# The first loads of a two-layer MoE and LoRA kernel: one queue in place of two, and 32 constant products ahead of the first real one in place of 27

## The chip, the cores and the metric

One core of one Trainium2 chip runs the kernel. The metric is the device time in microseconds (us); lower is better. Where several runs are given, the middle one counts.

## What is computed

`x` has 2 samples of 1024 tokens and 256 channels, in float32. Two layers are added to it one after the other. The first is a mixture of experts: per sample the router takes the 2 best of 8 experts, each an MLP with gelu and a hidden size of 1024, and a shared MLP is added. The second is a linear layer with a low-rank part, mixed from 8 pairs of matrices.

```python
def mlp(x, g, u, d):
    return (gelu(x @ g) * (x @ u)) @ d          # 256 -> 1024 -> 256, tanh gelu

w, sel = top_k(softmax(cond_8), 2)              # one row per sample
w = w / w.sum(-1)
x = x + sum(w[e] * mlp(x, skill_gate[e], skill_up[e], skill_down[e]) for e in sel) \
      + mlp(x, shared_gate, shared_up, shared_down)
x = x + x @ W_base.T + b_base + 2.0 * sum(cond_8[e] * (x @ As[e].T) @ Bs[e].T for e in range(8))
```

## The kernel before

The work on TensorE is done in float32 split into two parts: a high part rounded to the matmul's type (`hi_of`, L177) and the rest (`lo_of`, L180). Each product of two float32 matrices is then three matmuls, high by high, low by high and high by low, summed in PSUM. The first layer is cut into groups: for each of the 2 samples and each of its 3 MLPs (shared, first expert, second expert) there are 4 pieces of 256 hidden units, 24 groups in all. In a group the gate and the up matrix are each a matrix of 2 by 2 blocks (A11, A12, A21, A22), and so is the sample's x (B11, B12, B21, B22; the second index is the half of the tokens). Groups 1 to 23 use a scheme with seven block products in place of eight (`block_product`, L288). Group 0 uses the plain eight (`plain_product`, L299), because they need no sums of blocks before TensorE can begin: first A11 with B11 into the banks ps_ag and ps_au (six matmuls of 128x512, gate and up in turn), then A21 with B11 into ps_dg and ps_du (six), then A12 and A22 with the second block of x, which is named P2, and so on with B12 and P3. After gelu and the product with the up half, `down` (L346) multiplies by the down weights and sums into four banks `y`.

The order of all work is written by hand. `at` (L105) puts a step with a time into a list, `MOVED` shifts single steps by their place in the list, and L621 sorts by time and place and issues them. Each engine then runs its steps in exactly that order. So the time of a step is only its place in the queues of the engines it uses: a load's place is that on SP's or ACT's queue of DMA issues, which are also in the order of the engine's other work.

The steps at about -30 are the beginning. `warm_up` (L430) issues `WARM` matmuls of 128x128 on a constant tile of ones, into a bank of `y` that is not in use yet. `gelu_table` (L172) runs one small activation on ACT so that its table of functions is loaded. `load_first` (L205) loads a piece of group 0's weights from a packed copy: block A11 (columns 0 to `G2`, 128 KB), then A21 (`3 * G2`), A12, A22, and at last the down weights (256 KB). `load_x` (L249) loads one block of x (256 KB): (0, 0) is B11, (1, 0) the one named P2, (0, 1) is B12 and (1, 1) is P3. In the kernel before, B11 is issued by ACT, ahead of the table load, and all others by SP. `load_w` (L193) loads group 1's weights (768 KB). At -1.0 and after it come the splits that the first products need: A11's high part on ACT (L178), its low part on DVE (L181), then B11's high and low part on DVE, then A21's and A12's in the same manner, then P2's.

Of the kernel before, what the change touches and what calls it, by code (L numbers as in the profile page):

```python
# [67 lines left out]
MOVED = {  # L68
    33: -9.6, 40: 1.5, 81: -2.9, 87: -31.6, 100: 6.0, 101: 5.6, 102: 1.2, 1584: 7.5, 1599: 3.6, 1605: 8.7,
}  # L70
WARM = 27
LEN = 22


# [13 lines left out]
def moe_then_lora(ctx: ExitStack, tc: tile.TileContext, x, cond, skill, shared, piece0, second, outT):  # L88

    nc = tc.nc  # L90
# [14 lines left out]
    def at(t, f, *args):  # L105
        plan.append((round(t + MOVED.get(len(plan), 0), 1), len(plan), f, args))
# [139 lines left out]

    xraw, xs = {}, {}

    def load_x(b, k, j, eng=nc.sync):  # L249
        xraw[b, k, j] = xr_ring.next()  # L250
        eng.dma_start(out=xraw[b, k, j], in_=x[b, j, k])

    def x_sum(b, i, eng):

# [174 lines left out]
    def warm_up():  # L429
        ones = nc.const_aps.tensor(1.0, [P, P], BF16)  # L430
        for _ in range(WARM):
            nc.tensor.matmul(y[0][0][:, 0:P], lhsT=ones, rhs=ones, start=True, stop=True)

    V, A, G = nc.vector, nc.scalar, nc.gpsimd
    at(-30, warm_up)
    at(-29.9, gelu_table)
    at(-30, load_first, 0, G2)
    at(-30, load_x, 0, 0, 0, A)
    at(-29.8, load_first, 3 * G2, 4 * G2)
    at(-29.7, load_first, G2, 2 * G2)  # L440
    at(-29.6, load_x, 0, 1, 0)
    at(-29.5, load_first, 2 * G2, 3 * G2)
    at(-29.4, load_x, 0, 0, 1)
    at(-29.3, load_x, 0, 1, 1)
    at(-29.25, load_first, 4 * G2, PW)
# [153 lines left out]
    b = B - 1  # L599
# [90 lines left out]
```

## Time and profile before

| what | value |
|---|---|
| median of 3 runs | 383.97 us (383.63, 383.97, 385.43) |
| the profiled execution's own time | 385.71 us |
| its span, from the first to the last instruction | 383.9 us |
| TensorE busy (PE) | 378.6 us, 99% of the span |
| VectorE busy (DVE) | 296.2 us, 77% |
| ScalarE busy (ACT) | 255.7 us, 67% |
| GpSimd busy (POOL) | 199.5 us, 52% |
| constant products (L432) | 27, from 0.76 us on |
| first real product (L307) | at 4.99 us |
| B11's load: issue on ACT's queue | 0.72 us, 0.40 long |
| A11's load: issue on SP's queue | 0.72 us; landed 2.90 later |

The profiled execution is one run, looked at closely by the hardware profiler; its times are in us from its first instruction. A line of the timeline has the start, the length, the engine, the line of the kernel, the operation, the tiles (what is written, then what is read), their size and the count; in brackets is how long the engine stood idle before it, and what ended that. PEld is TensorE's loading of the stationary operand, SPq and ACTq are the issues of DMAs on SP's and ACT's queue. A line "A <- B" among the waits says that A stood idle until B was done.

### The profile page before, as it was taken

To read this page: it belongs to the slowest core of one execution; us is meant where nothing else is said; L and a number is where in the kernel's file an instruction comes from. 1 tells how busy PE (TensorE), PEld (TensorE's weight loads), DVE (VectorE), ACT (ScalarE), POOL (GpSimd) and SP (SyncE) were. 2 spreads that over 40 slices of the span, in tenths; PEclk is the share of its full clock that TensorE was granted. 3 is DMA by queue.
4 is the path that set the end of the run, shared out by engine and by line. 5 is a ranking of instruction groups with operands and counts; after the bars stand their busy time and mean duration, and the time that the engine had idled before them with its cause. 6 is when DMAs were issued, how large, how long until landed. Compare 5 with 4: busy or idle time off the path is not lost.

```text
span 383.9 us, 4871 instructions
## 1 busy us (share of the span) xinstructions
PE 378.6 (99%) x1689; PEld 313.9 (82%) x1689; DVE 296.2 (77%) x421; ACT 255.7 (67%) x439; POOL 199.5 (52%) x215
## 2 busy tenths in 40 slices
PE   7999999999999999999999999999999999999996
PEld 6888888888888888888888888888888888888885
DVE  4998897687876899877798887668668668677586
ACT  3678886767766767857858767667668567576520
POOL 0566788777465474555545664654655555340100
PEclk9999999999999999999999999999999999999999
DMA  7621221120220222031241202202202202000014
GB/s 248 247 55 56 82 84 14 68 84 0 84 82 1 85 82 82 2 137 29 109 164 28 85 0 82 82 2 82 82 2 83 82 2 83 0 2 0 0 56 164
DMA packets 8087, 26.00 MB, mean 68 GB/s; under 512 B 1024, under 2 KB 2048, under 8 KB 8064
## 3 DMA queue, kind: packets, MB, share of 16 engines
q0 software_dynamic: 2304, 12.58, 10.2%
q1 hardware_dynamic: 5616, 12.86, 9.7%
q8 instruction: 13, 0.21, 0.2%
q10 hardware_dynamic: 144, 0.26, 0.2%
q14 instruction: 10, 0.08, 0.1%
HBM read 23.60 MB, written 2.10 MB: 67 GB/s over the span
## 4 chain that ended last, share of the span: by engine, by line
PE 98%; DMA 1%; DVE 0%; ACT 0%; issue 0%
PE y L356 34%; PE ps_au L285 17%; PE ps_ag L285 17%; PE ps_dg L285 13%; PE ps_du L285 13%; PE ps_dg L307 1%; PE ps_du L307 1%; DMA w_raw<-in_piece 1%; PE y L307 1%; PE ps_ag L307 1%; PE ps_au L307 1%; PE ps_dg L379 0%; DVE ge L424 0%; DVE wa L181 0%; ACT wa L178 0%; DVE x L178 0%
## 5 line engine op out<-in xcount | busy, mean ns | idle before, releaser
L356 PE MATMUL y<-acts,wd 128*128 128x512 f32 x576 | 146.3, 389 | 0.0
L356 PEld LDWEIGHTS y<-acts,wd 128*128 128x128 f32 x576 | 108.0, 188 | 22.4
L181 DVE TENSOR_TENSOR acts<-act,acts 128x512 fp32r<-128x512 f32 x96 | 66.2, 722 | 12.2 <-ACT acts L178 12.2
L181 POOL TENSOR_TENSOR wa<-w_raw,wa 128x512 fp32r<-128x512 f32 (+1 forms) x46 | 53.7, 1182 | 36.3 <-PE ps_dg L285 32.3
L220 POOL TENSOR_TENSOR sf<-w_raw 128x256 f32<-128x256 f32 x46 | 39.3, 855 | 52.5 <-ACT u_u L311 26.6
L178 ACT CAST acts<-act 128x512 fp32r<-128x512 f32 x96 | 57.6, 620 | 13.0 <-DVE act L334 8.2
L181 POOL TENSOR_TENSOR wd<-w_raw,wd 128x256 fp32r<-128x256 f32 x44 | 32.2, 752 | 52.7 <-ACT wd L178 52.5
L317 DVE TENSOR_TENSOR c_u<-ps_du,u_u 128x512 f32<-128x512 f32 x46 | 31.6, 686 | 32.3 <-PE ps_du L285 31.0
L334 DVE SCALAR_TENSOR_TENSOR act<-ge,gate_w,c_u 128x512 f32<-128x512 f32 x48 | 45.3, 943 | 3.4 <-ACT ge L326 1.4
L326 ACT ACTIVATE ge<-c_g 128x512 f32<-128x512 f32 x69 | 43.7, 634 | 1.2 <-DVE c_g L317 0.3
L311 ACT COPY u_u<-ps_au 128x512 f32<-128x512 f32 x46 | 27.0, 588 | 26.1 <-PE ps_au L285 26.1
L285 PE MATMUL ps_au<-x,ws 128*128 128x512 f32 x138 | 38.8, 389 | 0.0
L285 PE MATMUL ps_dg<-x,ws 128*128 128x512 f32 x138 | 38.8, 389 | 0.0
L285 PE MATMUL ps_du<-x,ws 128*128 128x512 f32 x138 | 38.8, 389 | 0.0
L285 PE MATMUL ps_ag<-x,wa 128*128 128x512 f32 x138 | 38.8, 389 | 0.0
L285 PE MATMUL ps_au<-x,wa 128*128 128x512 f32 x138 | 38.8, 389 | 0.0
L285 PE MATMUL ps_ag<-x,ws 128*128 128x512 f32 x138 | 38.8, 389 | 0.0
L317 DVE TENSOR_TENSOR c_g<-ps_dg,u_g 128x512 f32<-128x512 f32 x46 | 31.5, 684 | 9.2 <-ACT ws L178 4.6
L326 ACT ACTIVATE ge<-ps_ag 128x512 f32<-128x512 f32 x24 | 14.4, 599 | 35.6 <-PE ps_ag L285 34.0
L285 PEld LDWEIGHTS ps_dg<-x,ws 128*128 128x128 f32 x138 | 25.9, 188 | 5.4
L285 PEld LDWEIGHTS ps_au<-x,ws 128*128 128x128 f32 x138 | 25.8, 188 | 5.5 <-ACT u_u L311 0.2
L285 PEld LDWEIGHTS ps_ag<-x,ws 128*128 128x128 f32 x138 | 25.9, 188 | 5.4
(105 smaller groups left out, 558.7 us busy)
## 6 DMA issues: line engine op xcount, KB each, us to landing
w_raw<-in_shared SPq DMA_DIRECT2D x7, 768.0 KB, 4.4
xr<-in_x SPq DMA_DIRECT2D x15, 256.0 KB, 3.0
lora_in<-in_second SPq DMA_DIRECT2D x1, 514.0 KB, 5.1
w_raw<-in_piece SPq DMA_DIRECT2D x4, 128.0 KB, 3.1
outT<-u_g SPq DMA_DIRECT2D x2, 256.0 KB, 2.0
outT<-u_u SPq DMA_DIRECT2D x2, 256.0 KB, 2.0
outT<-ge SPq DMA_DIRECT2D x4, 128.0 KB, 1.7
xr<-in_x ACTq DMA_DIRECT2D x1, 256.0 KB, 3.1
```

The lines of the kernel that those rows point to most:

```text
L178: (eng.copy if eng is nc.scalar else eng.tensor_copy)(pair[:, 0, :], src)
L181: eng.tensor_tensor(pair[:, 1, :], src, pair[:, 0, :].bitcast(F32), ALU.subtract)
L220: eng.tensor_tensor(ssum(i), a, b, op)
L285: nc.tensor.matmul(ps, lhsT=l, rhs=r, start=(start and n == 0), stop=(n == len(parts) - 1), skip_group_check=True)
L307: nc.tensor.matmul(plain_bank[ij, h], lhsT=w[:, wp, c:c + P], rhs=x[:, xp, :], start=(k == 0 and n == 0), stop=(n == 2), skip_group_check= ...
L311: nc.scalar.copy(part[m, h], bank["a", h])
L317: nc.vector.tensor_tensor(sums[g, h, ij], bank["d", h], part[m, h], ALU.add)
L326: nc.scalar.activation(ge[g, ij], result(g, 0, ij), AF.Gelu_apprx_tanh)
L334: nc.vector.scalar_tensor_tensor(act[g, ij], ge[g, ij], gate_w[:, s - 1, b:b + 1], result(g, 1, ij), ALU.mult, ALU.mult)
L356: nc.tensor.matmul(y[j][c], lhsT=w[:, wp, o:o + P], rhs=a[:, ap, :], start=first and n == 0, stop=last and n == 2, skip_group_check=True)
```

## The change

Three things in the first steps, and nothing else:

- B11's load goes from ACT's queue to SP's, with -29.9 in place of -30, so that it is issued second there, behind A11 (-30) and ahead of A21 (-29.8). `load_x` loses its argument for the engine.
- `gelu_table` goes from -29.9 to -30. ACT's queue then begins with the table load.
- `WARM` is 32 in place of 27.

```diff
-WARM = 27
+WARM = 32
...
-    def load_x(b, k, j, eng=nc.sync):
+    def load_x(b, k, j):
         xraw[b, k, j] = xr_ring.next()
-        eng.dma_start(out=xraw[b, k, j], in_=x[b, j, k])
+        nc.sync.dma_start(out=xraw[b, k, j], in_=x[b, j, k])
...
     at(-30, warm_up)
-    at(-29.9, gelu_table)
+    at(-30, gelu_table)
     at(-30, load_first, 0, G2)
-    at(-30, load_x, 0, 0, 0, A)
+    at(-29.9, load_x, 0, 0, 0)
     at(-29.8, load_first, 3 * G2, 4 * G2)
     at(-29.7, load_first, G2, 2 * G2)
```

On every engine the order of the other instructions is the same as before: on SP's queue the later loads move one place back, on ACT's one issue is gone, on TensorE five pairs of weight load and matmul come first.

## The prediction

> **What bounds the kernel now.** I read first the chain of work that ended last. The second line is its split by engine, in shares of the span:
>
> ```profile
> ## 4 chain that ended last, share of the span: by engine, by line
> PE 98%; DMA 1%; DVE 0%; ACT 0%; issue 0%
> ```
>
> TensorE (PE) is the bound from its first real product to the end: whatever makes that product earlier, or the products after it shorter, comes off the time one for one, and nothing else does unless it makes PE wait. The waits of PE confirm that there are only two (us in total, times, longest):
>
> ```profile
> PE ps_ag L307 <- DVE x L178: 1.2, 1, 1.2
> PE y L432 <- PEq L679: 0.8, 1, 0.8
> ```
>
> So the change, which touches only the first microseconds, is read from the chain there (start us, length us, what):
>
> ```profile
> 0.72 2.90 DMA w_raw<-in_piece
> 3.62 0.02 issue
> 3.64 0.41 ACT wa L178
> 4.06 0.02 issue
> 4.08 0.42 DVE wa L181
> 4.51 0.35 DVE x L178
> 4.85 0.14 issue
> 4.99 0.77 PE ps_ag L307
> ...
> 9.17 0.42 PE ps_du L307
> 9.59 0.23 PE ps_dg L307
> ```
>
> The first product starts at 4.99: A11 lands at 3.62, ACT makes its high part, DVE its low part, DVE then rounds B11 (x), then PE goes. Up to about 9.4 a product takes 0.43 us, after that 0.23: TensorE ran at half rate for its first ten to eleven products. The page's clock row shows full clock there; its record of the granted clock in the trace begins only at 9.45 us, so the spacing is what tells. The cost of that stretch: from 4.99 to 9.39 ten products took 4.40 us, at 0.2275 they take 2.28, so 2.1 us, and 2.15 with the half-slow eleventh.
>
> The third view is the timeline of the same stretch (start, length, what):
>
> ```profile
> 0.72 0.40 ACTq L251 DMA_DIRECT2D xr<-in_x  x1
> 0.72 1.33 SPq L208 DMA_DIRECT2D w_raw<-in_piece  x3
> 0.76 3.04 PE L432 MATMUL y<-const-bfloat16-1.0 128*128 128x128 bf16 x27 [0.76 <-PEq L679]
> 4.42 0.42 DVE L178 CAST x<-xr 128x512 fp32r<-128x512 f32 x1
> 7.42 0.43 DVE L178 CAST x<-xr 128x512 fp32r<-128x512 f32 x1 [1.18 <-DMA xr<-in_x]
> ```
>
> The 27 constant products keep PE busy from 0.76 to 3.80; then it has nothing for 1.19 us. B11's load was issued by ACT at 0.72 and landed 3.1 us later, at 3.82, so DVE's cast at 4.42 did not wait for it (no idle is shown before it): the cast stood behind A11's low part.
>
> **What the Trainium skill says.** "TensorE: Matmul & The Clock Gate", Part 1 (What's actually happening): the array starts at half rate and goes to full rate after a busy window of 3.41 us on a grid that runs free of the kernel; the note there says that one kernel therefore saw 6, 11 or 14 slow matmuls. The trace agrees on the grid: its clock record lasts 375.466 us, 110.0 windows of 3.413. Windows thus ended at 9.45, 6.04 and 2.63 in this run. In the one from 2.63 to 6.04 PE worked until 3.6 (the last constant started at 3.49, one lasts 0.107) and from 4.99: 2.0 of 3.41, or 60%, and it did not lift the clock; the full one after it did. How full is full enough the page doesn't state; its 6 slow matmuls, if of 0.43 us, are 2.6 us or 75% of a window, so I estimate the limit at 70% (60 to 75).
> "DMA: Bandwidth & Descriptors", Issuing engines are not separate DMA queues: loads from SP and ACT run on the same 16 engines and interleave; a second issuer saves only issue time. Agrees: the ACT issue took 0.40, one on SP 0.43, and the packets of A11 and B11 alternate in the records from 1.95 to 3.2 us. The same page, Queues, rings and completion order: an engine alternates between queues, and takes one queue's packets in order. So A11 in front on the one queue no longer shares its engines with B11.
>
> **The change, part by part.** The profiled execution took 385.71 us (span 383.9 and 1.8 around it); the median of the runs is 383.97, 1.74 lower. The three runs are 383.63, 383.97 and 385.43. I read this as the free grid: two runs had little or no half-rate stretch, one and the profiled one had it. 385.71 - 2.15 = 383.56, beside 383.63, fits. With a limit of 70% (2.39 us), the first window that can pass ends 2.39 us after PE's first work at 0.82, at 3.21; the last that passes on the constants alone ends at 4.62; so 1.41/3.41 = 41% of starts are warm at once, the others turn warm at 8.0 to 10.0. That gives two clusters some 2 us apart, as seen.
>
> *Five more constant products.* 5 x 0.107 = 0.54 us more of PE: their end goes from 3.80 to 4.33, into time in which PE waits. They cost nothing unless the first product could start before 4.33. They shrink the hole in PE's work from 1.19 to 0.4 us (with the start below), so any window that holds the hole is 80 to 90% full and passes. The clock then rises between 3.21 and 6.62, evenly over that window, in place of before 4.62 or at 8.0 to 10.0. With a start of 4.7: 56% of starts have a slow rest of up to 1.92 us, which costs 0.47 us each us (0.2 of 0.43): 0 to 0.9, mean 0.25.
>
> *A11 alone in front.* Its 128 packets ran from 1.74 to 3.26 among B11's. Lower bound of its landing: without B11's 84 ns packets between its 46 ns ones, up to 0.6 us earlier; upper bound: unchanged, since the engines were not full before 2.5 us[...]. I take 0.3: ACT at 3.35, DVE's low part at 3.8, the cast of B11 at 4.1.
>
> *B11 behind it.* Issued 0.43 later (1.15 for 0.72), but now ahead of A21 without alternation; by 3.82 the engines had moved A11, B11 and most of A21 anyway, and the first two still come first. Landing 3.5 at the earliest, 4.8 at the latest (1.9 us from its first packet to landing, as before, begun only when A11's packets are out at 2.9); I take 4.0. Then the cast starts at about 4.1 to 4.15, ends at 4.55 and PE starts at 4.7 with the same 0.14 of delay: -0.3 us, bounds -0.7 (but never before 4.33) and +0.6.
>
> *Every load behind it on SP* (A21, A12, the second x block, A22, two more x blocks, down weights, group 1's weights) is issued one slot, 0.43 us, later. From 2.5 us on the engines are mostly full and the sum of bytes is the same, so most land less than that later. Covers: P1 feeds 12 products; at full rate from 4.7 PE wants P2 at 7.4. Its x block landed at 7.40 here, but 15 of 16 engines had it by 5.91, one engine had stuck on a packet of 1.44 us; at 6.3 it gives P2's high part at 6.8. Cost 0; if an engine sticks again, 7.4 + 0.4 + 0.43 of cast is 0.8 us of waiting. A21's high part is wanted at 6.1 and was there at 4.56; A22's wanted at 8.8, landing about 6.7. The next to be late would be P2.
>
> *ACT's issue removed.* ACT starts its table load at about 0.75 in place of 1.15, and ends at 2.2; it then waits for A11 as before (0.99 us of idle ahead of 3.64). Nothing.
>
> Sum against the profiled execution: 385.71 - 2.15 - 0.3 + 0.25 = 383.5, with 382.9 to 384.7 from the bounds. Against the median, whose runs seem to have been warm already, that is 0.5 us, 0.1%: below the 0.5% that a measurement of this kernel can tell from no change. What it does is take away the slow cluster.
>
> **The rivals.** *The half-rate stretch was in all runs.* Then the 1.74 us between profile and median belong to profiling, and the runs differ for other reasons: 383.97 - 2.15 - 0.3 + 0.25 = 381.8. For it: the one trace that can be looked at has the stretch. Against it: 385.43 without a profile, and the fit of 383.56 to the lowest run.
> *The constants do nothing:* only a window without a hole lifts the clock. Then the stretch lasts 3.4 to 6.8 us from the first product before and after, and only the start moves: 383.97 - 0.3 = 383.7. For it: the 60% window failed, and a hole of 0.4 remains; against it: 6 slow matmuls on the page are less than a window.
> *Slower: B11 comes late.* It decides once B11 lands after 4.42, where DVE takes it now: from there each us is a us of PE. At its upper bound of 4.8 to 5.0 the cast ends at 5.4, PE starts at 5.55 (+0.6), the hole is 1.2 us again and the clock's luck as before: 384.6, and 386 with an unlucky clock. For it: the later issue and the serial queue; against: the two loads together are 384 KB, moved by 3.3 in either order.
>
> **How the numbers follow.** Likeliest case 0.50 (383.5; own range 382.9 to 384.7), stretch in all runs 0.25 (381.8), constants without effect 0.13 (383.7), B11 late 0.12 (384.6). Faster by over 0.5% is below 382.05: the second case, 0.25. Slower by over 0.5% is above 385.9: the unlucky part of the last case, 0.05. The rest, 0.70, is within. The range takes in the second case and the end of the last: 381.6 to 384.8.
>
> **What would show it.** Right: ACT's first cast before 3.64 (about 3.35); 32 constants ending near 4.3; the first product at 4.4 to 4.9; products of 0.43 us gone by 6.6 at the latest; no PE wait at P2 above 0.3. Wrong: DVE idle on the x load ahead of its first cast (B11 late), products of 0.43 after 6.7 (a hole of 0.4 still empties the window), or all runs near 382 (the stretch was always there).

## The result, and the profile after

| | before | after |
|---|---|---|
| median (22 runs each) | 385.55 us | 384.17 us |
| lowest, highest | 383.63, 386.03 | 383.66, 384.90 |
| profiled execution, its span | 385.71, 383.9 | 384.11, 382.3 |
| constants end / first product | 3.80 / 4.99 us | 4.34 / 4.75 us |
| granted clock record begins | 9.45 us | 6.04 us |

The ratio is 0.9971, with a 95% interval of 0.9962 to 0.9980: 0.3% less time, inside the 0.5% that was called no change, but clear of the noise in these runs. (A second sample of the same kernel, e8 below, is less clear.) The median of before that the prediction used, 383.97, came from three runs, two of which were among the fastest of the kernel; over 22 runs it is 385.55. The lowest times of the two kernels are the same. What went away is the upper end.

The times of before fall in two groups, with nothing between 384.6 and 384.7 us. Below, a run is called early when it lies in the lower group of its sample, late when in the upper one. Of the 22 runs of before 3 are early; of those made beside the experiments 17 of 59 (e1 to e4, median 385.31), 11 of 39 (e5 to e7, 385.30) and 15 of 34 (e8 and e9, 385.07). That is 46 of 154, or 30%. (The recorded texts call a TensorE at its full clock, or a run in which the clock rose early, warm.) Each ratio below is against the runs of before that were made beside it. Where a sample falls in two groups, the ratio need not follow its median.

The chain at the start, after (start us, length us, what), answers to the chain shown of before:

```profile
0.73 0.38 SPq L208
1.11 0.06 issue
1.17 2.99 DMA xr<-in_x
4.16 0.02 issue
4.18 0.44 DVE x L178
4.62 0.14 issue
4.75 0.76 PE ps_ag L307
5.52 0.43 PE ps_au L307
5.94 0.33 PE ps_ag L307
6.28 0.23 PE ps_au L307
```

B11 now stands on the path in place of A11, the first product is 0.24 us earlier, and only two products and a part of the third go at half rate. The timeline of the same kernel (start, length, what, idle before it) shows A11 and the constants:

```profile
0.77 3.57 PE L432 MATMUL y<-const-bfloat16-1.0 128*128 128x128 bf16 x32 [0.77 <-PEq L679]
2.75 0.40 ACT L178 CAST wa<-w_raw 128x256 fp32r<-128x256 f32 x1 [0.53 <-DMA w_raw<-in_piece]
4.18 0.43 DVE L178 CAST x<-xr 128x512 fp32r<-128x512 f32 x1 [0.57 <-DMA xr<-in_x]
6.60 0.43 DVE L178 CAST x<-xr 128x512 fp32r<-128x512 f32 x1
```

A11 had landed by 2.73, 0.89 earlier than before (ACT's cast 2.75 for 3.64); B11 landed at 4.16, 0.34 later. DVE waits for it (0.57). P2's cast at 6.60 waited for nothing.

With the products of the two traces set side by side in order, the profiled execution after is 0.24 us ahead at the first, 1.74 at the eighteenth, and 1.58 from about the eightieth to the end. The 1.74 are 0.24 of start and 1.50 of half-rate stretch; 0.17 are given back. The place is in group 1 (timeline, after):

```profile
18.55 0.62 ACT L178 CAST ws<-sf 128x512 fp32r<-128x512 f32 x1 [0.52 <-POOL sf L220]
...
19.07 0.59 ACT L326 ACTIVATE ge<-ps_dg 128x512 f32<-128x512 f32 x1
...
19.71 0.54 PEld L285 LDWEIGHTS ps_dg<-x,wa 128*128 128x128 f32 x3 [0.25 <-ACT ge L326]
19.72 0.97 PE L285 MATMUL ps_dg<-x,wa 128*128 128x512 f32 x3
```

The product of group 1 into bank ps_dg at 19.72 needs group 0's last gelu to have read that bank; its three matmuls take 0.97 us in place of 0.84. The gelu stands on ACT behind a cast that waits for GpSimd's sums.

### The profile page after: what moved, and what is told of

Read it like the earlier page. It is cut to its first block, busy times and chain, and to the rows that moved or that the text cites. A ratio compares the mean times of both kernels' runs of the same rounds, so it can differ in the third digit from the quotient of the medians.

```text
span 382.3 us, 4882 instructions
## 1 busy us (share of the span) xinstructions
PE 377.8 (99%) x1694; PEld 313.3 (82%) x1694; DVE 297.1 (78%) x421; ACT 255.6 (67%) x439; POOL 200.6 (52%) x215
## 4 chain that ended last, share of the span: by engine, by line
PE 98%; DMA 1%; DVE 0%; SPq 0%; issue 0%
PE y L356 34%; PE ps_au L285 17%; PE ps_ag L285 17%; PE ps_dg L285 13%; PE ps_du L285 13%; DMA xr<-in_x 1%; PE ps_du L307 1%; PE ps_dg L307 1%; PE y L307 1%; PE ps_ag L307 1%; PE ps_au L307 0%; PE ps_dg L379 0%; DVE ge L424 0%; DVE x L178 0%; SPq L208 0%
## 5 line engine op out<-in xcount | busy, mean ns | idle before, releaser
L181 DVE TENSOR_TENSOR acts<-act,acts 128x512 fp32r<-128x512 f32 x96 | 67.4, 735 | 12.2 <-ACT acts L178 11.9
L285 PEld LDWEIGHTS ps_au<-x,wa 128*128 128x128 f32 x138 | 25.9, 188 | 5.4
```

Source lines behind the costliest of these rows:

```text
L181: eng.tensor_tensor(pair[:, 1, :], src, pair[:, 0, :].bitcast(F32), ALU.subtract)
L285: nc.tensor.matmul(ps, lhsT=l, rhs=r, start=(start and n == 0), stop=(n == len(parts) - 1), skip_group_check=True)
```

## The experiments

The theory: TensorE's clock rises at the end of a fixed window of 3.41 us that is full enough, on a grid that has nothing to do with the kernel. The hole between the constants and the first product decides whether a window passes, and the change shrinks that hole from both sides. The rivals: the gain is the earlier first product alone, or the constants count one by one without a limit. A second question came out of the trace: why are the fastest runs not faster?

**e1: 32 constants alone.** The loads as before.

```diff
-WARM = 27
+WARM = 32
```

> 32 constants with the loads as before. The constants end at about 4.3 us, the first product stays at 5.0, so the hole in TensorE's work is 0.65 to 0.75 us, where it was 1.2 (before) and 0.4 (after). Theory of the clock (a window of 3.41 us that is about 80% busy lifts the clock, the 22 runs of before fit 0.79 to 0.82): the fill of a window with the whole hole is 78 to 80%, right at the limit, so either nearly all runs are warm by 7 us (median 384.3 to 384.6, ratio about 0.997) or 60% of them turn warm only at 8 to 10 us (median 385.0). Theory of the start (the gain is the earlier first product): no change, 385.5.

Measured: median 385.09 (14 runs), ratio 0.9991 (0.9976 to 1.0007). Seven runs lie at 383.73 to 384.71, seven at 385.48 to 386.04, with nothing in between. Its profile is one of the upper ones: hole 0.67, clock record from 9.58 us. The second branch of the expectation, then, with half of the runs early and not 40%.

```profile
0.76 3.57 PE L432 MATMUL y<-const-bfloat16-1.0 128*128 128x128 bf16 x32 [0.76 <-PEq L679]
5.00 0.77 PE L307 MATMUL ps_ag<-x,wa 128*128 128x512 f32 x1 [0.67 <-DVE x L178]
```

**e2: the queue alone.** The loads as after, `WARM = 27`.

> The loads as after, 27 constants. The constants end at 3.8, the first product is at 4.75, the hole is 0.95 to 1.15 us, a fill of 66 to 72%. Theory of the clock: a window with the hole does not lift the clock, so products of 0.43 us last until 8 to 10 us in four runs of five, and the median is that of before less the start, 385.3 (ratio 0.999). Theory of the start: most of the gain of after is here, about 384.3.

Measured: median 384.90 (22 runs), ratio 0.9999 (0.9986 to 1.0012). Eight runs at 383.54 to 384.33, the other 14 at 384.76 to 385.87. So neither half of the change, e1 or e2, can be told from no change, while both together gave 0.3% in their first 22 runs. The start alone should have given 384.3 here. (In e2's one profile the first product came at 4.97, hardly earlier than before, because B11 landed only at 4.38; the new order starts it anywhere from 4.52 to 4.97 in its eight profiles, the old one at 4.92 to 5.00 in three.) The share of early runs, 8 of 22, is more than the fifth that was expected; the runs of before beside it have 17 of 59.

**e3: no constants.** The loads as after, `WARM = 0`.

> The loads as after and no constant product at all. TensorE first works at 4.75. Theory of the clock with a limit of 80%: the clock rises between 7.5 and 10.9 us, mean 9.2, so 2.1 us of loss on average, some 385.4, spread from 384.6 to 386.2; about equal to before, that is, 27 constants bought nearly nothing in before in four runs of five. Theory of the start: as after, 384.2.

Measured: 385.42 (14 runs, 384.53 to 386.21), ratio 1.0007 (0.9993 to 1.0021); clock record from 9.05. As the theory of the clock said, nearly to the run. Its first product came at 4.61, earlier than in the profile after, and nothing was gained: that refutes the theory of the start. Beside e2, which differs in the constants alone, it has no early run where e2 has 8 of 22, and a median 0.5 us higher. So 27 constants with a hole of 1.2 us bought something in about a third of the runs, and nothing in the others.

**e4: 36 constants.** The loads as after, `WARM = 36`.

> 36 constants with the loads as after: they end at 4.76 in the records, where the first product starts, so the hole is closed. Theory of the clock with a limit (a window needs some 80%): the hole of after already passes, so nothing more is gained, 384.2, ratio to after 1.000. Rival (a fuller window is lifted sooner, any hole costs): the clock rises earlier, 383.8. If the constants delay the first product, it is up to 0.1 us later.

Measured: 384.11 (22 runs, 383.57 to 384.96), ratio 0.9977 (0.9967 to 0.9988). The hole is closed (PE shows no wait ahead of its first product) and nothing more is gained than with 32. That fits a limit, and not a sum.

**e7: 29 constants.** The loads as after, `WARM = 29`, between e2 and after.

> The loads as after with 29 constants: they end at about 4.0 in the records (array work to 3.9), the first product is at 4.5 to 5.0, so a window with the whole hole is some 68 to 82% full, mostly below the limit, which the profiles of the runs so far put between 78% (did not lift the clock) and 85% (did). Theory of a limit: two clusters again, a third or more of the runs near 384, the others at 384.7 to 385.8; median 384.5 to 385. Rival (every constant counts alike): a straight line between 27 constants (384.9) and 32 (384.2), 384.6 in one cluster, without runs above 385.2.

Measured: 384.39 (22 runs), ratio 0.9986 (0.9974 to 0.9998). Two groups again: 14 runs at 383.64 to 384.65 and 8 at 385.13 to 385.79. The rival of a straight line has the median about right, but not the gap in the middle nor the eight runs above 385.1. With 27, 29 and 32 constants the share of late runs, each counted from its sample's own gap, goes 14 of 22, 8 of 22, 0 of 22. No late run of e2 or e7 was profiled, and a late second x block puts a run at the same place without any help of the clock (e5 and e8 below). It is not likely to have made all eight of e7's: of the 89 runs with the new order and 32 or 36 constants (after, e4, e5, e8, e9) 5 lie above 385.0.

All profiles together give the limit. For each, the window that ended where the clock record begins, and the one or two before it, with the share of it in which PE worked (constants counted as 0.107 us each from the first to the last start, products from the first on):

| kernel | windows that did not lift the clock | window that did | clock from, us |
|---|---|---|---|
| before | 55%, 59% | 100% | 9.45 |
| e1 | 58%, 74% | 100% | 9.58 |
| e3 | 0%, 30% | 100% | 9.05 |
| e9 (below) | 43% | 81% | 5.63 |
| after | 54% | 82% | 6.04 |
| e2 | | 83% | 3.97 |
| e6 (below) | | 83% | 3.97 |
| e7 | 4% | 85% | 4.31 |
| e5 (below) | 13% | 86% | 4.61 |
| e8 (below) | 5% | 94% | 4.34 |
| e4 | 55% | 100% | 6.06 |

Nothing up to 74% lifted it, everything from 81% did. Where the limit lies depends on the count: with the constants taken to their recorded ends, as in the expectations of e1 and e7, e1's window is 80% full and e9's 87%. That the grid is free of the kernel shows in after and e8, which are the same code: the record begins at 6.04 in one and at 4.34 in the other.

**e5: group 0's last gelu ahead.** The profile of e2 happens to be a run with full rate from the first product. Its chain of waits runs not along TensorE but here (start, length, what):

```profile
4.95 6.48 DMA w_raw<-in_shared
11.44 0.07 issue
11.51 1.87 POOL sf L220
13.38 1.75 POOL wa L181
15.13 1.16 POOL sf L220
16.28 0.07 issue
16.35 1.13 POOL sf L220
...
17.56 1.07 POOL sf L220
18.63 0.02 issue
18.66 0.02 ACT ws L178
18.68 0.50 issue
19.18 0.60 ACT ge L326
19.78 0.04 issue
19.82 0.96 PE ps_dg L285 x3
```

Group 1's weights land at 11.44, GpSimd works its sums until 18.63, ACT casts the last two, then does the gelu, and PE, which was ready at 19.35, starts that product at 19.82 and is some 0.6 us behind after it. The edit lets the gelu go first; it changes nothing else in the order of any engine:

```diff
-    at(20.0, split_ws, 1, 2, 4, hi_of, A)
+    at(20.15, split_ws, 1, 2, 4, hi_of, A)
```

> The kernel after, with group 0's last gelu ahead of the second cast of group 1's sums in ACT's order. Theory of the floor (a start that is early enough runs into group 1: its weights land at about 11.9, GpSimd's four sums end at 18.6, ACT casts the last two and only then does the gelu that frees the bank which TensorE needs at 19.1 to 19.7): the waits of 0.1 to 1.0 us at that product go, the fastest runs get faster by 0.3 to 0.4 (lowest 383.2 to 383.3 in place of 383.6) and the median by 0.2 to 0.5, to 383.7 or 383.9. Rival (the fastest runs are just those with a full-rate start, nothing stands behind it): no change, 384.2 and lowest 383.6.

Measured: 383.86 (10 runs, 383.44 to 385.02), ratio 0.9960 (0.9946 to 0.9973). The median is as expected, the lowest run not as low. The slowest run is the profiled one, and shows another wait (its waits of PE, then its timeline):

```profile
PE ps_ag L307 <- DVE x L178: 1.7, 2, 1.1
```

```profile
8.43 0.43 DVE L178 CAST x<-xr 128x512 fp32r<-128x512 f32 x1 [2.30 <-DMA xr<-in_x]
...
9.01 0.47 PE L307 MATMUL ps_ag<-x,wa 128*128 128x512 f32 x1 [1.13 <-DVE x L178]
```

The second x block (P2) landed at 8.41, and PE had nothing to do for 1.1 us after its twelfth product. Of the 16 parts in which the landing of a block is reported, 15 had come by 6.36; the last came 2.05 us later. One packet of 2 KB that was under way then took 2.23 us, from 5.29 to 7.52, where most of its size take 0.084; the trace does not say to which load it belongs. The median is 0.31 us below the first 22 runs of after, but the runs of before beside it are 0.25 us below theirs too, so this run does not settle what the exchange is worth.

**e6: the same exchange in the kernel before.**

> The kernel before with that same exchange of two ACT instructions. Theory of the floor: most runs of before reach group 1 some 2 us later and never wait there, so the median stays within 0.1% (385.3), while the few runs with an early clock fall below 383.5. Rival (the order costs something in itself): a gain in all runs as in the kernel after.

Measured: 385.55 (14 runs), ratio 0.9995 (0.9981 to 1.0010): nothing in the median, as the theory of the floor said; three runs at 383.54 to 383.83, not below 383.5. The profiled run is one of these, with full rate from the first product at 4.92, as in e2's. PE reaches the same place in group 1 at 19.10 in e6 and 19.12 in e2; two products on it is at 19.56 and 20.16; the last product of all starts at 378.10 and 378.73. So the wait costs 0.6 us in a run like e2's. But it is not the exchange that spared e6 the wait (timeline of e6):

```profile
16.31 1.25 POOL L220 TENSOR_TENSOR sf<-w_raw,sf 128x256 f32<-128x256 f32 x1
...
17.43 0.59 ACT L326 ACTIVATE ge<-ps_dg 128x512 f32<-128x512 f32 x1
...
17.92 0.61 ACT L178 CAST ws<-sf 128x512 fp32r<-128x512 f32 x1
...
19.33 0.84 PE L285 MATMUL ps_dg<-x,wa 128*128 128x512 f32 x3
```

GpSimd's last sum ended at 17.56 here and at 18.63 in e2. In the old order the second cast could have started at about 17.6, and the gelu would have ended at about 18.7 (an estimate from the 0.5 us between two ACT instructions and the gelu's 0.6), ahead of PE, which came at 19.3. In keeping with that, the fastest runs of the kernel before without the exchange are as fast as e6's: 383.58 in the 59 runs beside e1 to e4. Why GpSimd was a microsecond later in e2 (its first sum took 1.87 us, in e6 0.89) is open.

**e8 and e9: after, and after with the gelu ahead, side by side.** e8 is the kernel after without an edit, e9 is e5's kernel.

> The kernel after, unchanged, on the chip and in the rounds of the next run, to set that one beside it. All theories: 384.0 to 384.3.

> The kernel after with group 0's last gelu ahead of the second cast, again, beside the kernel after itself. Theory of the floor: 0.2 to 0.4 us below the kernel after in the median (the wait at group 1's second product is 0.1 to 1.0 us in the profiles of warm starts), with single runs as slow as 385 where the second x block comes late; its ratio to before 0.996 against 0.997. Rival (the exchange does nothing, the first sample of ten runs was lucky): the same ratio as the kernel after, medians within 0.1 us.

Measured: e8 384.33 (14 runs, 384.01 to 386.02), ratio 0.9993 (0.9979 to 1.0008); e9 383.80 (21 runs, 383.19 to 384.44), ratio 0.9973 (0.9963 to 0.9984). The median of e8 is where it was expected, but four of its runs lie at 385.4 to 386.0, which none of the first 22 did. The slowest of them was profiled:

```profile
PE ps_ag L307 <- DVE x L178: 1.8, 2, 1.4
PE y L432 <- PEq L679: 0.8, 1, 0.8
PE ps_dg L285 <- ACT ge L326: 0.7, 1, 0.7
```

It had its full clock before the first product (record from 4.34), lost 1.4 us to P2's block, which landed at 8.53, and 0.7 to the gelu. So a late block eats what the clock gave. Whether the other three runs had the same cause is not shown. The interval of e8's ratio takes in 1: in this second sample the change by itself cannot be told from no change, with 4 late runs of 14 against 19 of 34 in the kernel before.

In e9's profile the exchange can be seen at work (its timeline on ACT, then on PE):

```profile
18.70 0.59 ACT L326 ACTIVATE ge<-ps_dg 128x512 f32<-128x512 f32 x1
19.32 0.62 ACT L178 CAST ws<-sf 128x512 fp32r<-128x512 f32 x1
```

```profile
19.65 0.84 PE L285 MATMUL ps_dg<-x,wa 128*128 128x512 f32 x3
```

GpSimd's last sum ended at 19.28. The gelu, now ahead of the cast that waited for it, was done at 19.29 and PE's product at 19.65 did not wait; behind the cast the gelu could have started at about 19.8 at the earliest. e9 is 0.53 us below e8 in the median, and 0.4 if e8's four late runs are left out: the exchange is worth some 0.4 to 0.5 us on top of the change in this pair, and e9's lowest run, 383.19, is the lowest of all. The intervals of the two ratios overlap a little. e9's ratio is no better than the one that the change had in its first 22 runs: the runs of before that stood beside it had a median of 385.07.

## Why the prediction was right or wrong

It gave 383.5 (381.6 to 384.8) and no change that can be told as the likeliest; 384.17 came, with a gain of 0.3%. That "no change" held is in part luck: its base was 1.6 us too low and its end 0.67 too low, and the two errors pull the gain in opposite directions. By its own steps:

- **TensorE is the bound, and the start and the half-rate stretch are what counts.** Right. Start and stretch gave 1.74 us in the two profiles.
- **The clock rises on a free grid, and a fixed fill of a window is needed.** Right in kind: e1 to e4, e7 and the table of windows. The limit of 70% was too low; by its own count it lies between 74 and 81%. Hence "41% of starts are warm at once" was too many: 46 of 154 runs of before are early. The same sum gives 30% for a limit of 76% (an estimate, and in that bracket). The 6 slow matmuls that the estimate of 70% rested on need not have been matmuls of 0.43 us.
- **Two of the three runs of before were warm, as 385.71 - 2.15 = 383.56 fits.** It fits, and misled: no early run of before was profiled, but e6's, with the same loads and constants and full rate from its first product, took 383.54. The three were not typical. The forecast of "no change" stood on their median; against 385.55, 383.5 would have been 0.5%.
- **Five more constants cost nothing and shrink the hole to 0.4.** Right: 0.42, in e4 even 36 cost nothing. Spread of the kernel after: 383.66 to 384.90, 1.2 us, where a slow rest of 0 to 0.9 us was worked out; in e8 four runs lie above that.
- **A11 0.3 us earlier, B11 at 4.0, start at 4.7.** A11 was mis-sized (0.89; the bound was 0.6 us), B11 was 4.16, the start 4.75, and 4.52 to 4.97 over all profiles with the new order. A11's surplus was of no use, since B11 ends last.
- **The later loads cost nothing; P2's block would cost 0.8 us if an engine sticks.** Right as a case, and under-sized: 1.1 us of waiting in e5's profile, 1.4 in e8's. The packet of 1.44 us on which it laid P2's late landing at 7.39 cannot be the cause: it ran from 6.31 to 7.75. What the trace before shows is 15 of 16 parts of the block by 5.91 and the last at 7.39.
- **The sum of 383.5.** It is 0.67 too low against the median, and 0.6 against the profiled execution, 384.11, where the sum can be gone through: the start gave 0.24 and not 0.3; the slow rest was 0.65 (2.15 less the 1.50 gained) and not the mean of 0.25, within the 0 to 0.9 that it allowed; and 0.17 were lost in group 1. That last term was missing: the sum takes it that everything behind group 0 has room for a start that is 2 us earlier. It looked only as far as P2 and found that "the next to be late would be P2". The next, where P2 was on time, was group 1's chain from its weights' landing over GpSimd's sums to the gelu. It takes most from the runs with the earliest clock: 0.17 us in the profile after, 0.6 in e2's. e9 without that wait has a median of 383.80. The remaining 0.3 us of the median are not divided up by any run.
- **Rivals.** "The half-rate stretch was in all runs" (381.8) is out: no run came near. "The constants do nothing" is out by the profiles, where windows with a hole in them lifted the clock (82% full in after, 81% in e9), and by e2 against after. "B11 comes late" did not happen: it lands before 4.42 in all profiles with the new order (3.81 to 4.38).

## What to carry to other kernels

Filling work that is there to raise TensorE's clock must reach close enough to the real work: here no window up to 74% full lifted the clock and every one from 81% did, so two edits, neither of which could be told from nothing alone, gave 0.3% together in their first sample. When the runs of a kernel fall in two groups, a median of three can land in either: take enough runs to know the share of each group, and take them again, since here the share of early runs of one kernel went from 3 of 22 to 15 of 34. And after taking time out of the start, look for the first wait behind it that does not move with it, here a load that lands when it lands and an order of two ACT instructions behind it.

## What the runs showed of the hardware that was not expected

- A11's load of 128 KB, in front of B11's on the same queue, landed 2.0 to 2.2 us after its issue (eight profiles); with B11's 256 KB beside it on another queue, 2.8 to 2.9 (three).
- Some packets of 2 KB took 0.6 to 2.2 us where most take 0.084, at other places in every profile. P2's block of 256 KB landed at 7.38, 7.40, 8.41 and 8.53 us in four profiles, at 6.03 to 6.73 in the other seven. In the three latest, 15 of its 16 parts had come 1.5 to 2.1 us before the last. That a slow packet held up the last one is likely and not shown.
- The clock record began 110.0 or 111.0 windows of 3.413 us before its end in all eleven profiles.
